# Scan layer: transposed input, ScalarE fills the bank of B, GpSimd keeps the states, a rewritten unit table

## The chip, the cores and the metric

The kernel runs on one core of one Trainium2 chip, and everything below is about that core. It has five engines that work side by side and wait for each other through semaphores: TensorE (PE; PEld is its weight load), VectorE (DVE), ScalarE (ACT), GpSimd (POOL) and SyncE (SP). In this kernel SP issues every DMA, so its queue is the order of all transfers. Matrix products are written to PSUM, which has 8 banks of 2 KB for each of 128 partitions; all else lives in SBUF and in device memory. The metric is the device time of one execution in microseconds (us).

## The reference

The input x has 8 sequences of 1024 rows of 256 numbers, all in float32. The computation, cut to what matters:

```
hs, res = split(x @ w_in.T)                      # 512 + 512 channels
u  = silu(causal_conv(hs, 4 taps))
dt, B, C = split(u @ w_xproj.T)                  # 64, 16, 16
delta = softplus(dt @ w_dt.T + b_dt)
z_t = exp(delta*A) * z_(t-1) + (delta*u) * B_t   # 512 channels x 16 states
y  = sum over states (z * C) + u*D
x1 = layernorm(x + (y * silu(res)) @ w_out.T)

q, k, v = x1 @ W_qkv + b_qkv                     # 16 heads of 16
attn = softmax(q k.T / 4) v
gate = softmax(x1 @ W_gate + b_gate); the two largest of 8 experts
moe  = sum over chosen experts of gate_e * (x1 @ W_e + b_e)
out  = layernorm(x1 + attn + moe)
```

## The kernel before

There are two parts, one after the other. `scan_moe_layer` computes everything but the attention and leaves `acc` (x1 plus experts), q and k (split in an upper half `hi` and a remainder `lo`) and v in device memory. `attention_layer` reads them. The change lies in the first part alone, and line numbers below are those of the kernel before.

**Steps, quads, slots.** The scan part works in 16 steps; a step is half a sequence, 512 rows. In a step there are 4 chunks of 128 channels and 16 states; with them 128 partitions hold 4 groups of 32 channels, and a *quad* is one of 16 combinations of a chunk and a state group g (in the order 0, 2, 1, 3). A quad has four scans of 128x512 (r = 0 to 3). One scan is one *slot*, so a step has 64 slots. Steps come in pairs: in the opening step the states start at zero, and the last column of each quad is kept in `state` (L649) for the closing step.

**What a quad does.** ScalarE makes the exponentials `da`, two slots ahead (L570, three PSUM buffers). `times_b` multiplies the 128x2048 input `ex` by the rows of B: for g below 2 on VectorE (L579), with B in a PSUM bank `pb`; for the others on GpSimd (L581), with B in the SBUF tile `bt`. VectorE scans (L630). GpSimd multiplies by the rows of C, `ct` (`times_c`, L586), in place, so the last column must have been copied before. TensorE sums the states two quads later (L596), and at the end of a chunk VectorE applies the gate (L603). `pb` is filled by TensorE (`copy_b`, L545): a 0/1 matrix `rp` picks rows of B out of `xd`. `pb` has one buffer, so the product waits for the multiply that reads it. `bt` and `ct` are filled by DMAs that repeat one row over 32 partitions, four for each tile (`load_bc`, L555); their buffers are single, so a load waits for the last reader of the step before.

**The table of units.** Everything else is cut into units, each a few products into one of three PSUM banks and a *read* some slots later (mostly two), which empties the bank. `SLOTS` (L46) says which unit starts at which of the 64 slots; the order of instructions on PE, ACT, DVE and POOL is exactly that of the program, while SP's is set by a scheduler. Units of the next step: `ph`, `pc`, `px`, `pd`, `pr` (projections, convolution, rows of B and C, delta, gate) and `pt`, which transposes the rows of x by TensorE and ScalarE (L188, L197) for `ph` and `pr`. Units of the step before: `po` (output projection and row norm; GpSimd's part L320 to L323), `yt` (transpose of x1), `pg` (gate logits), `q`, `v`, `gt` and `bi` (gate weights transposed, expert bias), and `e0` to `e15` (experts, two at a time, L487), whose read adds the product times the gate weight `gcb` on VectorE (L495). The gate's path is: VectorE takes `gmx` from `pg` and ScalarE copies it to `lg` (L414, L415), ScalarE's four exponentials `gex`, VectorE's comparisons `gp` (L422), GpSimd (L427, L428), VectorE's count `grk` (L431), and GpSimd's `gcb` (L436), nine slots after `pg`. For q and k, ScalarE writes `hi` (L363) and VectorE `lo` (L364) in the same read.

Of the kernel before, what the change touches and what calls it, by code (L numbers as in the profile page):

```python
# [16 lines left out]
P = 128  # L17
# [28 lines left out]
SLOTS = """  # L46
ph1 e12 ph2 e13 ph3 e14 e15 po0
po1 po2 po3 - - pc0 pc1 -
- - - yt0 yt1 pr0 pr1 pg
- q0 q1 v0 v1 pc2 pc3 q2  # L50
- px0 px1 q3 e0 pd0 pd1 gt
- e1 bi0 e2 bi1 pd2 pd3 e3
- e4 e5 e6 - pr2 pr3 e7
- e8 e9 pt0 pt1 e10 e11 ph0
""".split()
# [3 lines left out]
def scan_moe_layer(  # L59
    ctx, tc, ident, x, w_in, w_conv, w_x, w_dt, b_dt, a_log, d_skip, w_out, sel, rep,  # L60
    w_gate, b_gate, w_exp, b_exp, w_qkv, b_qk, acc, qk, v,
# [40 lines left out]

    def load_x(i, tag):

        b, s = steps[i]
        pool = p1 if tag == "xp" else p2
        t = work[i][tag] = pool.tile([P, TT, H], F32, tag=tag, name=f"{tag}_{b}_{s}")
        nc.sync.dma_start(t, x[b, s * LT : (s + 1) * LT, :].rearrange("(t p) h -> p t h", p=P))

    load_x(0, "xp")  # L110

    wi = wp.tile([P, HK, 2 * DIN], F32, name="wi")
    nc.sync.dma_start(wi, w_in.rearrange("(k p) d -> p k d", p=P))

# [3 lines left out]
    sl = wp.tile([P, ND], F32, name="sl")  # L118
    nc.sync.dma_start(sl, sel)

    wx = wp.tile([P, CH, R + 48], F32, name="wx")
# [14 lines left out]
    nc.sync.dma_start(wo, w_out.rearrange("(c p) h -> p c h", p=P))  # L136

    rp = wp.tile([R + NS, 2, P], F32, name="rp")
    nc.sync.dma_start(rp[R : R + NS].rearrange("n g p -> n (g p)"), rep)

# [21 lines left out]
    nc.gpsimd.memset(one, 1.0)  # L162

    be = rp[0:NE].rearrange("n g p -> n (g p)")
    nc.sync.dma_start(be, b_exp)
# [16 lines left out]
    def bank(name):  # L182
        return ps_m.tile([P, LT], F32, tag="mm", name=name)

    def transposed(name, xt, k):
        pt = bank(name)
        for t in range(TT):
            nc.tensor.transpose(pt[:, t * P : (t + 1) * P], xt[:, t, k * P : (k + 1) * P], ident)  # L188
        return pt

    def unit_pt(i, k):

        o = work[i]
        pt = transposed(f"pt_{i}_{k}", o["xp"], k)
        if k == 0:
            o["xT"] = p1.tile([P, HK, LT], F32, tag="xT", name=f"xT_{i}")
        yield 2, lambda: nc.scalar.copy(o["xT"][:, k, :], pt)  # L197

# [136 lines left out]
    def unit_yt(i, k):  # L335

        b, s = steps[i]
        o = work[i]
        pt = transposed(f"yt_{i}_{k}", o["xf"], k)
        if k == 0:  # L340
            o["yT"] = p1.tile([P, HK, LT], F32, tag="yT", name=f"yT_{i}")

        def read():
            nc.scalar.copy(o["yT"][:, k, :], pt)

        yield 2, read

    def unit_q(i, n):

        b, s = steps[i]  # L350
        o = work[i]
        c, a = divmod(n, 2)
        pq = bank(f"pq_{i}_{n}")
        for k in range(HK):
            nc.tensor.matmul(  # L355
                pq, wr[:, k, a * H + c * P : a * H + (c + 1) * P], o["yT"][:, k, :], start=(k == 0), stop=(k == HK - 1)
            )

        def read():
            hi = p4.tile([P, LT], F32R, tag="st", name=f"hi_{i}_{n}")  # L360
            lo = p4.tile([P, LT], F32R, tag="st", name=f"lo_{i}_{n}")
            bias = bqk[:, a, c : c + 1]
            nc.scalar.activation(hi, pq, AF.Identity, bias=bias)  # L363
            nc.vector.scalar_tensor_tensor(lo, pq, bias, hi.bitcast(F32), ALU.add, ALU.subtract)  # L364
            for j, t in ((0, hi), (1, lo)):
                nc.sync.dma_start(qk[b][c][a, :, j, s * LT : (s + 1) * LT], t.bitcast(F32))

        yield 2, read

    def unit_v(i, t2):  # L370
# [22 lines left out]
    def unit_pg(i, _):  # L393
# [18 lines left out]

        def logits():
            nc.scalar.copy(lg, pg)  # L414
            nc.vector.tensor_reduce(mx, pg, AX.X, ALU.max, negate=True)  # L415

# [86 lines left out]

    ahead = {"pt": unit_pt, "ph": unit_ph, "pc": unit_pc, "px": unit_px, "pd": unit_pd, "pr": unit_pr}
    behind = {
# [5 lines left out]
    def slot(t):  # L511
        i, j = divmod(t, len(SLOTS))
        if j == 8 and 0 < i + 2 < NSTEPS:
            load_x(i + 2, "xp")
        if j == 2 and 0 < i <= NSTEPS:
            load_x(i - 1, "xf")
        for read in due.pop(t, ()):
# [4 lines left out]
        if name in ahead:  # L522
            m = i + 2 if name in ("pt", "ph") and j >= 56 else i + 1
            if 0 <= m < NSTEPS:
                reads = ahead[name](m, n)
        elif name in behind:

            m = i - 2 if name == "e" and j < 16 else i - 1
            if 0 <= m < NSTEPS:
                reads = behind[name](m, n)  # L530
        for later, read in reads:
            due.setdefault(t + later, []).append(read)

    def place(k):
# [4 lines left out]
    def copy_b(k):  # L541

        i, c, g, o = place(k)
        pb = quads["b", k] = ps_b.tile([P, LT], F32, tag="pb", name=f"pb_{k}")
        nc.tensor.matmul(pb, rp[R : R + NS, g, :], o["xd"][R : R + NS, :], start=True, stop=True)  # L545

    def load_bc(i, g):

        o = work[i]
        for a, tag in ((0, "bt"), (1, "ct")):  # L550
            if a == 1 or g > 1:
                t = o[tag, g] = p1.tile([P, LT], F32, tag=f"{tag}{g}", name=f"{tag}_{i}_{g}")
                for m in range(NM):
                    row = o["bc"][a, 4 * m + g : 4 * m + g + 1]
                    nc.sync.dma_start(t[ND * m : ND * m + ND], row.to_broadcast([ND, LT]))  # L555

# [49 lines left out]
    with tc.manual_schedule(engines={eng.PE, eng.Activation, eng.DVE, eng.Pool}):  # L606
# [3 lines left out]
        for g in ORDER:  # L610
            load_bc(0, g)
        load_chunk(0, 1)
        load_experts(0)
        copy_b(0)
        times_b(0)
        copy_b(2)
        times_b(1)
        exp(0)
        exp(1)
        for k in range(K + 2):  # L620
            i, cj = divmod(k, QUADS)
            if cj > 12 and i + 1 < NSTEPS:
                load_bc(i + 1, ORDER[cj - 13])
            if cj == 0 and 0 < i < NSTEPS:
                load_bc(i, ORDER[3])
            for r in range(NR):
# [17 lines left out]
                if r == 3:  # L644
                    if k % 2 == 0 and k + 4 < K:
                        copy_b(k + 4)
                    if k < K:
                        if steps[i][1] + 1 < NSTEP:
                            nc.scalar.copy(state[:, c, g, :], quads[k][:, :, LT - 1])  # L649
                        times_c(k)  # L650
                slot(NR * k + r)
        for t in range(NR * (K + 2), len(SLOTS) * (NSTEPS + 1) + 18):
            slot(t)
# [255 lines left out]
def tile_kernel(  # L909
    ctx: ExitStack, tc, x, w_in, w_conv, w_x, w_dt, b_dt, a_log, d_skip, w_out, sel, rep,  # L910
    w_qkv, b_qk, b_v, w_gate, b_gate, w_exp, b_exp, out,
# [12 lines left out]
    scan_moe_layer(  # L924
        tc, ident, x, w_in, w_conv, w_x, w_dt, b_dt, a_log, d_skip, w_out, sel, rep,
        w_gate, b_gate, w_exp, b_exp, w_qkv, b_qk, acc, qk, v,
# [42 lines left out]
```

## Time and profile before

| | |
|---|---|
| median of 4 runs (lowest to highest) | 4028.35 us (4009.29 to 4036.53) |
| the profiled execution | 4021.62 us, its span 4019.6 us |
| scan part | the first scan starts at 77.5 us, the last ends at 2103.2 us |
| one step, opening / closing | 127.4 / 128.6 us in the middle of the part |
| attention part | from about 2188 us to the end |

The page's first rows give busy time, share of the span and instruction count of each engine:

```profile
PE 3656.7 (91%) x15168; PEld 1399.0 (35%) x15168; DVE 3219.1 (80%) x3590; ACT 2329.2 (58%) x3146; POOL 2062.7 (51%) x817
```

These shares mix the two parts. The change is to be judged by the rows of the scan part alone, which a table by window gives. In a row of waits, "A <- B: 62.6, 39, 2.6" says that A's engine sat idle 62.6 us in total, 39 times, at most 2.6 us, and that B ended the idle time. A timeline row has start, duration, engine, line and tiles, and in brackets the idle time before it.

### The profile page before, as it was taken

The page shows a single profiled execution, that of the slowest core. Times are in us where ns is not written, and L with a number is a line of the kernel's source. Part 1 is how long each engine was busy: PE and PEld are TensorE (multiplying, and loading weights), DVE is VectorE, ACT ScalarE, POOL GpSimd, SP SyncE. Part 2 cuts the span into 40 slices and gives each one's busy share as a digit, 9 for nine tenths or more (in the row PEclk, how much of TensorE's full clock was granted, in tenths as well). Part 3 has the DMA queues.
Part 4 walks back from the last instruction along what each step waited for, and adds up shares of the span by engine and source line. Part 5 has one row for each costly group of instructions (what it writes and reads, how often), then busy time and mean ns, then how long its engine had stood idle before and what let it go on. Part 6 is the DMA issues. An engine that isn't in the chain of part 4 may idle for free.

```text
span 4019.6 us, 45008 instructions
## 1 busy us (share of the span) xinstructions
PE 3656.7 (91%) x15168; PEld 1399.0 (35%) x15168; DVE 3219.1 (80%) x3590; ACT 2329.2 (58%) x3146; POOL 2062.7 (51%) x817
## 2 busy tenths in 40 slices
PE   5789898998989989898887899999999999999997
PEld 1133333333333333333334233333333333333332
DVE  2888998989989999899984577777777767777774
ACT  3656656655565556655540366666666656666665
POOL 2998999889998989889981000101101010101011
PEclk7689998999998999998987699999999989999999
DMA  8677776877677777777633322323323232323220
GB/s 209 145 185 191 179 190 173 198 188 188 173 182 195 184 192 173 197 189 173 170 82 118 99 75 85 90 94 89 99 80 111 74 102 79 106 85 94 89 77 27
DMA packets 288473, 545.51 MB, mean 136 GB/s; under 512 B 50459, under 2 KB 143795, under 8 KB 288243
## 3 DMA queue, kind: packets, MB, share of 16 engines
q1 hardware_dynamic: 288242, 542.63, 52.1%
q8 instruction: 121, 1.98, 0.2%
q14 instruction: 110, 0.89, 0.1%
HBM read 431.26 MB, written 110.15 MB: 135 GB/s over the span
## 4 chain that ended last, share of the span: by engine, by line
PE 47%; ACT 13%; DVE 13%; POOL 11%; DMA 7%; issue 6%; SPq 2%; ACTq 0%; POOLq 0%; DVEq 0%
PE av L819 13%; ACT es L802 11%; PE sc L800 11%; DVE dz L630 8%; POOL dz L586 8%; PE sm L775 7%; PE pe L487 3%; DMA ex<-dl 2%; PE y L596 2%; PE pq L355 2%; DVE dz L579 2%; DVE xf L495 2%; DMA hx<-hd 2%; POOL dz L581 1%; PE pr L202 1%
## 5 line engine op out<-in xcount | busy, mean ns | idle before, releaser
L779 DVE TENSOR_REDUCE mh<-sm 128x2 f32<-128x1024 f32 x1024 | 1250.0, 1223 | 395.5 <-PE sm L775 376.7
L802 ACT ACTIVATE es<-sc 128x1024 f32<-128x1024 f32 x1024 | 1047.2, 1024 | 660.0 <-PE sc L800 626.2
L586 POOL TENSOR_TENSOR dz<-dz,ct 128x2048 f32<-128x2048 f32 x256 | 1159.6, 4535 | 141.4 <-ACT state L649 78.2
L570 ACT ACTIVATE da<-ex,am 128x512 f32<-128x512 f32 x1024 | 698.0, 688 | 536.1 <-DVE dz L630 529.2
L844 POOL TENSOR_TENSOR acc<-acc,ot 128x256 f32<-128x256 f32 x64 | 46.7, 730 | 1464.4 <-DVE ot L840 1464.4
L800 PE MATMUL sc<-qst,kst 66*128 66x512 f32 x2048 | 763.2, 456 | 22.0 <-DMA qst<-mr 16.7
L630 DVE TENSOR_TENSOR_SCAN dz<-da,state,dz 128x512 f32<-128x512 f32 x512 | 630.5, 1267 | 11.6 <-ACT da L570 11.6
L630 DVE TENSOR_TENSOR_SCAN dz<-da,dz 128x512 f32<-128x512 f32 x512 | 599.1, 1207 | 17.7 <-ACT da L570 15.4
L581 POOL TENSOR_TENSOR dz<-ex,bt 128x2048 f32<-128x2048 f32 x128 | 580.2, 4533 | 36.6 <-DMA ct<-bc 32.5
L775 PE MATMUL sm<-kmx,qmx 64*128 64x512 f32 x2048 | 526.2, 511 | 54.3 <-DMA qst<-qk 10.7
L819 PE MATMUL av<-es,vaug 128*32 128x512 f32 x4096 | 559.2, 618 | 0.0
L487 PE MATMUL pe<-we,yT 128*128 128x512 f32 x1024 | 504.2, 628 | 37.1 <-ACT du L277 16.7
L800 PEld LDWEIGHTS sc<-qst,kst 66*128 66x128 f32 x2048 | 311.7, 191 | 587.6 <-DVE mh L779 299.7
L596 PE MATMUL y<-dz,sl 128*32 128x512 f32 x2048 | 311.9, 684 | 57.7 <-POOL dz L586 57.7
L775 PEld LDWEIGHTS sm<-kmx,qmx 64*128 64x128 f32 x2048 | 196.1, 188 | 457.2 <-ACT es L802 246.8
L579 DVE TENSOR_TENSOR dz<-ex,pb 128x2048 f32<-128x2048 f32 x128 | 289.8, 2264 | 67.9 <-DMA bt<-bc 63.5
L487 PEld LDWEIGHTS pe<-we,yT 128*128 128x128 f32 x1024 | 188.9, 196 | 324.3 <-issue 234.5
L495 DVE SCALAR_TENSOR_TENSOR xf<-pe,gcb,xf 128x256 f32<-128x256 f32 x512 | 243.4, 476 | 38.1 <-PE pe L487 29.0
L545 PE MATMUL pb<-xd,rp 16*128 16x512 f32 x256 | 161.6, 714 | 91.9 <-DVE dz L579 91.9
L202 PE MATMUL pr<-xT,wi 128*128 128x512 f32 x256 | 133.3, 668 | 2.2 <-ACT du L277 2.2
L355 PE MATMUL pq<-yT,wr 128*128 128x512 f32 x256 | 134.7, 664 | 0.0
L596 PEld LDWEIGHTS y<-dz,sl 128*32 128x32 f32 x2048 | 43.3, 114 | 251.0 <-issue 147.1
(106 smaller groups left out, 2751.7 us busy)
## 6 DMA issues: line engine op xcount, KB each, us to landing
ex<-dl SPq DMA_DIRECT2D x256, 512.0 KB
hx<-hd SPq DMA_DIRECT2D x256, 256.0 KB
we<-in_w_exp SPq DMA_DIRECT2D x130, 256.0 KB
dl<-du SPq DMA_DIRECT2D x64, 512.0 KB
qmx<-qk SPq DMA_DIRECT2D x128, 256.0 KB
kmx<-qk SPq DMA_DIRECT2D x256, 128.0 KB
qst<-qk SPq DMA_DIRECT2D x256, 128.0 KB
kst<-qk SPq DMA_DIRECT2D x512, 64.0 KB
```

The source lines that it names most:

```text
L487: nc.tensor.matmul(pe, o["yT"][:, k, t * P : (t + 1) * P], weights[e2][:, k].rearrange("p e f -> p (e f)"), start=(k == 0), stop=(k == HK ...
L570: nc.scalar.activation(da, o["ex", c][:, r, 0, :], AF.Exp, scale=am[:, c, g, r : r + 1])
L579: nc.vector.tensor_mul(t, o["ex", c][:, :, 1, :], quads.pop(("b", k)).unsqueeze(1).to_broadcast(full))
L581: nc.gpsimd.tensor_mul(t, o["ex", c][:, :, 1, :], o["bt", g].unsqueeze(1).to_broadcast(full))
L586: nc.gpsimd.tensor_mul(t, t, o["ct", g].unsqueeze(1).to_broadcast([P, NR, LT]))
L596: nc.tensor.matmul(y[ND * r : ND * r + ND, :], sl, t[:, r, :], start=False, stop=True, skip_group_check=True)
L630: nc.vector.tensor_tensor_scan(t[:, r, :], da, t[:, r, :], 0.0 if steps[i][1] == 0 else state[:, c, g, r : r + 1], ALU.mult, ALU.add,)
L775: nc.tensor.matmul(s[:, hh, :], qt_[rows, t * P : (t + 1) * P], kt_[rows, kh * QB : (kh + 1) * QB], start=True, stop=True,)
L779: nc.vector.tensor_reduce(mh[:, :, t, kh], s, AX.X, ALU.max)
L800: nc.tensor.matmul(s[:, cols], kt_[:, hh, kt * P : (kt + 1) * P], qt_[:, hh, cols], start=True, stop=True)
L802: nc.scalar.activation(e, s, AF.Exp, scale=HD**-0.5)
L819: nc.tensor.matmul(av[32 * j : 32 * j + 32, :], va[:, kt, VW * h : VW * h + 32], es[hh][:, q * QB : (q + 1) * QB], start=(kt == 0), stop=( ...
```

## The change

1. The host passes x a second time, transposed (`x_t`). `xT` is loaded by one DMA of 512 KB for each step, at slot 56 of the step before (`load_xt`); the units `pt`, their 8 transposes and 2 ScalarE copies, and the tile `xp` are gone. The load of `xf` (the residual rows) stays.
2. `copy_b` is a ScalarE copy of a tile `bt` into `pb`. So `bt` exists for all four g, `load_bc` is called for one tile at a time, and eight more row DMAs are issued in a step (`LOADS`: B's g 0 at quad 11, B's g 1 and C's g 0 at quad 13, and so on). The copy stands at odd quads, two slots ahead of its multiply, where TensorE's product stood six slots ahead. `rp` is gone.
3. The last states are copied by GpSimd (`tensor_copy`) just ahead of its own `times_c`.
4. In `unit_q`, `lo` and the two stores come one slot after `hi`; the tiles are taken when the unit starts. In `unit_pg`, `gmx` comes ahead of `lg`.
5. The table is rewritten: e0 starts at slot 31 instead of 36, e1 to e12 two to six slots later, e13, e14, e15 at slots 11, 15 and 17 instead of 3, 5 and 6; the units q and v are spread over slots 25 to 41; `gt`, `bi0`, `bi1` go from 39, 42, 44 to 42, 50, 52.
6. `w_in` is loaded in two halves at the start, and the loads before the first scan are reordered.

```
 SLOTS = """
-ph1 e12 ph2 e13 ph3 e14 e15 po0
-po1 po2 po3 - - pc0 pc1 -
-- - - yt0 yt1 pr0 pr1 pg
-- q0 q1 v0 v1 pc2 pc3 q2
-- px0 px1 q3 e0 pd0 pd1 gt
-- e1 bi0 e2 bi1 pd2 pd3 e3
-- e4 e5 e6 - pr2 pr3 e7
-- e8 e9 pt0 pt1 e10 e11 ph0
+ph1 e10 ph2 e11 ph3 e12 - po0
+po1 po2 po3 e13 - pc0 pc1 e14
+- e15 - yt0 yt1 pr0 pr1 pg
+- q0 v0 q1 - pc2 pc3 e0
+- px0 px1 v1 q2 pd0 pd1 -
+- q3 gt e1 - pd2 pd3 e2
+- e3 bi0 e4 bi1 pr2 pr3 e5
+- e6 e7 - e8 - e9 ph0
...
+    def load_xt(i):
+        b, s = steps[i]
+        t = work[i]["xT"] = p1.tile([P, HK, LT], F32, tag="xT", name=f"xT_{b}_{s}")
+        nc.sync.dma_start(t, x_t[b, :, s * LT : (s + 1) * LT].rearrange("(k p) t -> p k t", p=P))
...
-    def unit_pt(i, k):
-        o = work[i]
-        pt = transposed(f"pt_{i}_{k}", o["xp"], k)
-        if k == 0:
-            o["xT"] = p1.tile([P, HK, LT], F32, tag="xT", name=f"xT_{i}")
-        yield 2, lambda: nc.scalar.copy(o["xT"][:, k, :], pt)
...
         def read():
-            hi = p4.tile([P, LT], F32R, tag="st", name=f"hi_{i}_{n}")
-            lo = p4.tile([P, LT], F32R, tag="st", name=f"lo_{i}_{n}")
-            bias = bqk[:, a, c : c + 1]
             nc.scalar.activation(hi, pq, AF.Identity, bias=bias)
+
+        def rest():
             nc.vector.scalar_tensor_tensor(lo, pq, bias, hi.bitcast(F32), ALU.add, ALU.subtract)
...
         yield 2, read
+        yield 3, rest
...
         def logits():
+            nc.vector.tensor_reduce(mx, pg, AX.X, ALU.max, negate=True)
             nc.scalar.copy(lg, pg)
-            nc.vector.tensor_reduce(mx, pg, AX.X, ALU.max, negate=True)
...
-        if j == 8 and 0 < i + 2 < NSTEPS:
-            load_x(i + 2, "xp")
+        if j == 56 and 0 < i + 2 < NSTEPS:
+            load_xt(i + 2)
...
-            m = i - 2 if name == "e" and j < 16 else i - 1
+            m = i - 2 if name == "e" and j < 24 else i - 1
...
+    LOADS = ((11, 0, 0), (13, 0, 2), (13, 1, 0), (14, 0, 1), (14, 1, 1), (15, 1, 2))
...
-        nc.tensor.matmul(pb, rp[R : R + NS, g, :], o["xd"][R : R + NS, :], start=True, stop=True)
+        nc.scalar.copy(pb, o["bt", g])
...
-            if cj > 12 and i + 1 < NSTEPS:
-                load_bc(i + 1, ORDER[cj - 13])
+            if i + 1 < NSTEPS:
+                for at, a, j in LOADS:
+                    if cj == at:
+                        load_bc(i + 1, a, ORDER[j])
...
-                    if k % 2 == 0 and k + 4 < K:
-                        copy_b(k + 4)
+                    if k % 2 and k + 3 < K:
+                        copy_b(k + 3)
                     if k < K:
                         if steps[i][1] + 1 < NSTEP:
-                            nc.scalar.copy(state[:, c, g, :], quads[k][:, :, LT - 1])
+                            nc.gpsimd.tensor_copy(state[:, c, g, :], quads[k][:, :, LT - 1])
                         times_c(k)
```

## The prediction

> **What bounds the kernel now.** I read the page's busy shares first, then busy time by window, then groups by line, the totals of waits, and the timeline of three engines. A step is 64 slots, one per scan; slot numbers below are places in the table. Steps come in pairs (opening, closing half of a sequence); one pair from the middle, then the 10 us in the opening one in which TensorE was granted half its clock:
>
> ```profile
> 1084.30:1211.70 127.40, 115.66 (x414) 47.35 (x413) 115.24 (x133) 78.46 (x133) 115.67 (x38) 0.93 0.76 186
> 1211.70:1340.30 128.60, 117.37 (x420) 47.26 (x419) 118.93 (x133) 76.88 (x117) 118.02 (x38) 0.93 0.75 186
> ...
> 1121.00:1131.30 10.30, 8.86 (x22) 3.16 (x23) 9.06 (x9) 8.69 (x18) 10.30 (x4) 0.50 1.05 212
> ```
>
> The columns are stretch, length, then busy PE, PEld, DVE, ACT, POOL, granted clock, DMA share, GB/s. Three engines are busy 115 to 119 of 128 us: VectorE idles 12.2 and 9.7 us a step, GpSimd 11.7 and 10.6, TensorE 11.7 and 11.2. ScalarE idles 50. So no engine's work can be cut for its own worth; what counts is whose waits end last. Waits over 12.5 steps (360 to 1960 us):
>
> ```profile
> POOL dz L586 <- ACT state L649: 67.4, 26, 4.2
> DVE lo L364 <- ACT hi L363: 62.6, 39, 2.6
> PE pb L545 <- DVE dz L579: 61.3, 12, 5.5
> ...
> DVE gmx L415 <- ACT lg L414: 31.4, 13, 3.3
> ...
> DVE xf L495 <- PE pe L487: 12.3, 23, 0.7
> ...
> ACT hi L363 <- PE pq L355: 10.3, 6, 1.7
> ```
>
> ```profile
> 1120.95 1.98 PE L545 MATMUL pb<-xd,rp 16*128 16x512 f32 x2 [4.58 <-DVE dz L579]
> ```
>
> VectorE waits 5.0 us a step for `hi` and 2.5 for `lg`, and no row names GpSimd. Both waits stand in slots 25 to 33, and ScalarE is late there because TensorE is: it sat still 4.58 us at slot 18 (the line above: the product into `pb` waited for VectorE's multiply), dropped to half clock, and ran `pr`, `pg`, `pq` late. GpSimd's waits are for VectorE.
>
> What the new table will lean on is GpSimd's run from the end of the scan of slot 27 (1268.2) to the gate weights `gcb`, and VectorE's run to slot 33 beside it:
>
> ```profile
> 1268.22 4.53 POOL L586 TENSOR_TENSOR dz<-dz,ct 128x2048 f32<-128x2048 f32 x1 [0.19 <-DVE gsm L426]
> 1272.70 0.73 POOL L427 TENSOR_TENSOR gp<-gp,lower 128x256 f32<-128x256 f32 x1
> 1273.51 0.72 POOL L428 TENSOR_TENSOR gp<-gp 128x256 f32<-128x256 f32 x1
> 1274.19 4.55 POOL L581 TENSOR_TENSOR dz<-ex,bt 128x2048 f32<-128x2048 f32 x1
> 1278.69 4.56 POOL L586 TENSOR_TENSOR dz<-dz,ct 128x2048 f32<-128x2048 f32 x1
> ...
> 1283.80 0.25 POOL L436 TENSOR_TENSOR gcb<-grk,gex 128x32 f32<-128x32 f32 x1
> ```
>
> ```profile
> 1279.99 2.26 DVE L579 TENSOR_TENSOR dz<-ex,pb 128x2048 f32<-128x2048 f32 x1
> 1284.41 0.75 DVE L364 SCALAR_TENSOR_TENSOR lo<-pq,bqk,hi 128x512 fp32r<-128x512 f32 x1 [2.16 <-ACT hi L363]
> ```
>
> `gcb` is there 16.0 us after that scan. VectorE reaches the end of slot 33's multiply at 1282.25, 14.1 us after it, of which 3.1 us are waits (2.53 for `hi`, 0.43 for an exponential): 11.0 us of work.
>
> **The change, part by part, for one step.**
>
> *TensorE loses work.* Gone are 8 `pb` products (two passes each, 1.05 to 1.12 us together: 8.7) and 8 transposes of x (two units of four, 0.66 to 1.12 each: 1.8): 10.5 of 116.5 us. Experts e13 to e15 now lie at slots 11, 15 and 17, in the very hole in which TensorE stood still. So `pg` should end about when VectorE asks for it at slot 25, and the 2.4 us wait there goes. What is late next is ScalarE, for the comparison of slot 26. From the end of the scan of slot 23 it needs an exponential 0.75, table load 1.28, two Silus 1.2, table load and exponential 1.97, `lg` 0.2, exponential 0.7 and the gate's four 1.1: 7.2. VectorE needs two scans 2.4, the multiply 2.2, `gmx` 0.1 and a scan 1.2, and is there at 5.8: it waits 1.4 us, against 0.3 now (`lg` behind `gmx` costs nothing, ScalarE comes later anyway). Gain 1.3.
>
> *`lo` one slot later.* The three large `hi` waits (2.3 to 2.6) disappear as such, because a scan and ScalarE's queue lie between. `pq`'s bank is held a slot longer and q0, q1 stand two slots apart, so the ring of three banks still turns.
>
> *e0 moves from slot 36 to 31*, its VectorE read from 38 to 33. That read needs `gcb`, which GpSimd's queue gives 16.0 us after the scan of slot 27; VectorE's work up to there is 11.0. So VectorE waits 5.0 us at slot 33 (5.6 in opening steps, with two state copies in the run). Queued behind it are all scans, hence ScalarE's exponentials and TensorE's q2. This takes the place of what the `hi` waits gave: today slot 33's `lo` ends 17.1 us after the scan of slot 27, in the new order e0 may start after 16.0 to 16.6. GpSimd in turn stands still 3.3 us from `gcb` to the scan of slot 35 (e0 0.9, two scans 2.4), now as then (3.56).
>
> *State copies to GpSimd.* 16 in each opening step. ScalarE pays 0.193 for one; on GpSimd I bound it by its cheapest and dearest rows of 128x4: 0.20 (L322) and 1.04 (L321). It is a plain copy, nearest to L320's 0.23, plus 0.07 between dependent instructions: 0.30. From `gcb` to `gcb` there are 8 of them, 2.4 us. GpSimd's stretch becomes 3.3 + 116.8 + 1.3 (small gaps) + 2.4 = 123.8. It loses the wait for ScalarE (5.4 us a step), but that was mostly VectorE's lateness passed on.
>
> *`pb` by ScalarE.* 8 copies of 128x512, between 0.58 (L197) and 0.69 (L570, which writes the same kind of bank); 0.65. Less 2 copies of `xT` and in the mean 8 state copies (2.7): +2.5 of 78 us, hidden by 50 idle. The copy stands two slots (2.4 us of scans) before its multiply; without that cover VectorE would pay 8 x 0.65 = 5.2. Its rows `bt` 0 and 1 are asked for at slots 44 and 52, ten slots ahead.
>
> *SP.* 8 more row DMAs of 0.45 us, 3.6 us. `xT` is issued behind `ct`'s load, which waits for GpSimd's product of slot 55 (SP sits 5.3 us for that now, until 1205.7); it would land near 1211 to 1212, and ph0 is due at about 1210.6: 0 to 1.5 us of TensorE's slack.
>
> *The clock.* The 5 us wait at slot 33 empties TensorE around slots 35 to 39 (`q2` waits for e0's bank, `pd` for `xd`); I count `y` 1.1, `q2` 2.0 and `pd` 1.0 in 6.8 us there. At slot 43 of odd steps now, 5.0 busy of 6.8 were followed by 3.4 us at half clock; at slot 17, 2.0 to 4.5 by 10 to 13.7 us. So I expect the dip to move rather than go. A 3.4 us dip costs 1.7 us of product time and, with about 2 us slack a row, 1.0 us of VectorE's time (0 to 2.7).
>
> The Trainium skill, "TensorE: Matmul & The Clock Gate", Part 1, says that the array falls to half rate after an idle window of about 3.4 us. The trace shows its unit of 3.41 us, but a dip with 5.0 of 6.8 us busy, which the rule would not give. By the rule there is no gap that long left and the sum would be 15 us lower; I follow the rows.
>
> *Sum of a step.* VectorE's work 117.1 (unchanged), waits 5.3 + 1.4 + 1.0 (clock) + 1.0 (what stays of 3.0 us of small waits: `pe` 1.5, exponentials 1.0, `y` 0.4) = 125.8, against 128.0: 2.2 less, and 2.0 above GpSimd's 123.8. Fifteen steps: -33.
>
> *Start.* Step 0 is GpSimd's (102.4 of 109.2 busy): 16 x 0.30 = +4.8. Eight more row loads stand before the second chunk, 0 to +3.7; the transposes and the split `w_in` save about 1.5 before the first store. +4.5 (0 to 8.5). *End.* Two more expert units after the last scan, 3.8 us, fall into a 4.4 us hole (waiting for the normalized rows at 2123): 0. The attention part is untouched.
>
> -28.5 on the profiled execution's 4021.6 is 3993; that execution lies 6.7 below the median of the runs, so 4000.
>
> **Rivals.**
> 1. *GpSimd paces it, slower.* If a state copy costs 1.04 + 0.07, the stretch is 3.3 + 118.1 + 8.9 = 130.3: +2.3 x 15 + 17.8 at the start, about 4080. It decides from 0.82 us a copy. The 0.20 to 0.24 of other small rows speak against it.
> 2. *No change.* The wait for `gcb` comes with a long dip: e1 late by 2.7 us instead of 1.0, GpSimd half a microsecond late at slot 27. Then 128 a step, about 4030. For it: from slot 11 to 27 GpSimd needs six products at 4.51, the row norms 1.75 and gaps, 29.2, with four copies 30.4; VectorE needs 16 scans 18.5, two multiplies 4.4, three experts 2.7, two `po` 1.9, the gate's 1.4, and waits 1.4: 30.3. GpSimd has no room.
> 3. *More gain.* No dip, no small waits: GpSimd's floor 123.8, with copies at 0.2 123.0: -63 to -75 and the start, 3955 to 3970. Against it: two engines that close rarely mesh.
> 4. *The move does nothing*, since `hi` waits for `pq`: the `lo` waits stay. They would be covered by the `gcb` wait.
>
> **How the numbers follow.** My case (3975 to 4015) 0.42, rival 3 0.10, rival 2 with 4 0.27, rival 1 and other ways to lose 0.21. Within 0.5% (20 us) is about what a measurement of this kernel can tell from none. Part of my case lies within it: faster 0.47, same 0.29, slower 0.24. The range 3948 to 4070 leaves out the end of rival 3 and the dear end of rival 1; the likeliest case's own is 3975 to 4015.
>
> **What would show it.** `xf` of e0 waiting about 5 us for GpSimd once a step; no wait of `gmx`; `gp` waiting over 1 us for `gex`; `lo` without waits; state copies of 0.2 to 0.3 us on GpSimd; the half clock at slots 35 to 43 instead of 17 to 25; steps of 125 to 126. I am wrong if the copies are dear, if `xf` doesn't wait at slot 33, or if TensorE's half clock stays at slot 17.

## The result and the profile after

The changed kernel takes 4046.8 us (median of 40 runs, 4012.8 to 4078.0), the kernel before 4025.0 in the runs beside it (66 runs, 4001.3 to 4087.7). The ratio is 1.0053, with a 95% interval from 1.0039 to 1.0066: half a percent slower, where 4000 was forecast. Runs more than 1.5% above the fastest of their kernel count in medians and ranges, but not in ratios.

The profiled execution spans 4033.9 us. Its first scan starts at 83.9 us (77.5 before) and its last scan ends at 2135.6 (2103.2 before). Of these 32.4 us, 6.4 come before the first scan, 4.4 in step 0, and 22.3 in steps 2 to 15 (step 1 gave 0.6 back). Behind the scan this execution then took 18 us less than the one before (1898 against 1916). This part varies by tens of microseconds from execution to execution (see the last section), so experiments are compared here by the last scan's end as well as by the time.

The windows of an opening and a closing step of the changed kernel (stretch, length, busy time of PE, PEld, DVE, ACT, POOL, granted clock, DMA share, GB/s; a step of the kernel before took 127.4 and 128.6 us at this place):

```profile
1106.00:1233.30 127.30, 107.78 (x391) 43.48 (x389) 115.06 (x133) 79.72 (x123) 118.03 (x53) 0.95 0.77 190
1233.30:1364.90 131.60, 113.29 (x394) 45.62 (x395) 118.53 (x132) 80.67 (x123) 118.15 (x39) 0.90 0.76 185
```

TensorE lost work (111.6 us busy a step, 116.2 before; means of steps 2 to 14), VectorE's is unchanged (116.6, 116.9), GpSimd's grew a little (118.2, 116.7). VectorE's idle time grew from 10.8 to 12.9 us a step (mean of steps 2 to 14), GpSimd's from 11.0 to 11.4. The totals of waits from 360 to 1960 us of the changed kernel (waiting instruction, what it waited for: us in all, times, longest):

```profile
DVE xf L488 <- POOL gcb L429: 61.5, 13, 5.2
PE pc L225 <- DMA hx<-hd: 53.7, 14, 7.8
...
DVE xf L488 <- PE pe L480: 39.0, 35, 3.7
POOL dz L576 <- DMA bt<-bc: 29.1, 8, 4.5
...
DVE xf L302 <- DMA xf<-in_x: 20.4, 10, 3.6
...
POOL dz L576 <- DMA ct<-bc: 17.1, 4, 4.9
...
DVE gp L415 <- ACT gex L412: 14.1, 13, 1.2
```

The first and the last line are the two waits that the prediction had put there; the waits of `lo` for `hi` fell from 62.6 to 6.2 us. The four lines that name `hx`, `xf`, `bt` and `ct` are loads, which the prediction had not priced (`hs`, the read of `ph`, is stored to device memory, and `hx` is loaded from there for the convolution `pc`): `pc` waited 5.7 us for `hx` before, GpSimd 11.2 for rows, and VectorE never for `xf`.

### The profile page after: what moved, and what is told of

It reads as the page before. It is cut to its first block, busy times and chain, and to the rows that moved or that the text cites. A ratio compares the mean times of both kernels' runs of the same rounds, so it can differ in the third digit from the quotient of the medians.

```text
span 4033.9 us, 44586 instructions
## 1 busy us (share of the span) xinstructions
PE 3543.7 (88%) x14784; PEld 1356.9 (34%) x14784; DVE 3215.3 (80%) x3590; ACT 2367.2 (59%) x3114; POOL 2084.2 (52%) x945
## 4 chain that ended last, share of the span: by engine, by line
PE 37%; POOL 22%; ACT 13%; DMA 11%; DVE 8%; issue 6%; SPq 3%; ACTq 0%; POOLq 0%; DVEq 0%
POOL dz L581 13%; PE av L819 13%; ACT es L802 11%; PE sc L800 10%; PE sm L775 7%; POOL dz L576 6%; DVE dz L630 6%; DMA ex<-dl 4%; DMA hd<-hs 3%; DMA hx<-hd 2%; PE pe L480 2%; POOL du L266 1%; DVE xf L488 1%; PE pr L190 1%; SPq L550 1%
## 5 line engine op out<-in xcount | busy, mean ns | idle before, releaser
L630 DVE TENSOR_TENSOR_SCAN dz<-da,dz 128x512 f32<-128x512 f32 x512 | 596.9, 1206 | 13.7 <-ACT da L565 11.3
L480 PE MATMUL pe<-we,yT 128*128 128x512 f32 x1024 | 520.4, 640 | 9.0 <-issue 2.5
L225 PE MATMUL pc<-hx,cw 128*32 128x512 f32 x512 | 82.7, 744 | 99.3 <-DMA hx<-hd 83.0
L348 PE MATMUL pq<-yT,wr 128*128 128x512 f32 x256 | 141.8, 681 | 22.7 <-ACT du L265 12.3
L190 PE MATMUL ph<-xT,wi 128*128 128x512 f32 x256 | 130.8, 639 | 34.2 <-DMA xT<-in_x_t 18.3
```

What stands on the lines that cost most here:

```text
L480: nc.tensor.matmul(pe, o["yT"][:, k, t * P : (t + 1) * P], weights[e2][:, k].rearrange("p e f -> p (e f)"), start=(k == 0), stop=(k == HK ...
L630: nc.vector.tensor_tensor_scan(t[:, r, :], da, t[:, r, :], 0.0 if steps[i][1] == 0 else state[:, c, g, r : r + 1], ALU.mult, ALU.add,)
```

## The predicted chain at slot 33

VectorE's and GpSimd's timelines of the changed kernel around slot 33 of a closing step (start, length, instruction, idle time before it and its releaser):

```profile
1302.92 2.26 DVE L574 TENSOR_TENSOR dz<-ex,pb 128x2048 f32<-128x2048 f32 x1
1309.99 1.00 DVE L488 SCALAR_TENSOR_TENSOR xf<-pe,gcb,xf 128x256 f32<-128x256 f32 x2 [4.81 <-POOL gcb L429]
```

```profile
1294.12 4.57 POOL L581 TENSOR_TENSOR dz<-dz,ct 128x2048 f32<-128x2048 f32 x1 [1.52 <-DVE gsm L419]
...
1309.70 0.25 POOL L429 TENSOR_TENSOR gcb<-grk,gex 128x32 f32<-128x32 f32 x1
1313.43 4.51 POOL L581 TENSOR_TENSOR dz<-dz,ct 128x2048 f32<-128x2048 f32 x1 [3.48 <-DVE dz L630]
```

The scan of slot 27 ends at 1294.05. `gcb` is there 15.9 us later (16.0 forecast), VectorE's work up to slot 33 ends 11.1 us later (11.0 forecast), and GpSimd then stands still 3.48 us (3.3 forecast). The state copies are cheap; the group of the changed kernel (nanoseconds: least, median, most):

```profile
L649 POOL COPY state<-dz x128: 177/187/217, 90.7 to 2016.3; 128x4 f32<-128x4 f32 x128
```

The product into `pb` is gone from TensorE, and its wait of 4.58 us at slot 18 with it. What TensorE stands for at about the same place now, in the changed kernel's timeline:

```profile
1270.05 1.94 PE L225 MATMUL pc<-hx,cw 128*32 128x512 f32 x8 [7.03 <-DMA hx<-hd]
```

So the parts of the forecast that came out of compute rows hold here to 0.2 us. The miss is elsewhere.

## Experiments

Starts and ends (us) are from one profiled execution of each kernel; times and ratios are from its runs, against the kernel before run beside it (medians of 4025 to 4029). Set against the kernel before, the ratio turned into microseconds and the last scan's end agree to 15 us in every row (changed kernel 21 and 32), so a few microseconds between single ends decide nothing.

| kernel | first scan | last scan's end | time, median | ratio, 95% interval |
|---|---|---|---|---|
| before | 77.5 | 2103.2 | 4025.0 | 1 |
| changed | 83.9 | 2135.6 | 4046.8 | 1.0053 (1.0039 to 1.0066) |
| x1: xf early | 83.4 | 2113.2 | 4037.3 | 1.0030 (1.0005 to 1.0056) |
| x2: xf and xT early | 81.7 | 2111.5 | 4036.7 | 1.0018 (0.9994 to 1.0042) |
| x3: e0 later | 83.0 | 2089.0 | 4004.8 | 0.9940 (0.9921 to 0.9960) |
| x4: state copies on ScalarE | 83.0 | 2115.5 | 4038.6 | 1.0027 (1.0003 to 1.0051) |
| x5: x2 and rows apart | 84.9 | 2091.5 | 3998.0 | 0.9937 (0.9909 to 0.9965) |
| x6: x5 and e0 later | 83.6 | 2057.4 | 3972.5 | 0.9851 (0.9814 to 0.9889) |
| x7: before, lo later | 78.4 | 2115.4 | 4031.1 | 1.0015 (0.9986 to 1.0045) |
| x8: changed, old table | 82.8 | 2130.4 | 4051.6 | 1.0065 (1.0041 to 1.0089) |
| x9: x6, state copies on ScalarE | 84.6 | 2051.6 | 3973.5 | 0.9860 (0.9819 to 0.9901) |
| x10: changed, pb by TensorE | 79.7 | 2129.4 | 4043.2 | 1.0057 (1.0036 to 1.0077) |
| x11: before, rows apart | 76.7 | 2095.3 | 4020.8 | 0.9987 (0.9966 to 1.0008) |
| x12: before, xT alone | 81.2 | 2099.4 | 4020.8 | 0.9984 (0.9955 to 1.0012) |
| x13: changed, rows apart | 82.3 | 2096.4 | 4023.1 | 0.9986 (0.9953 to 1.0018) |
| x14: x6, other start | 83.1 | 2047.6 | 3966.8 | 0.9868 (0.9833 to 0.9903) |

Two theories stood first. G: the 4.7 us wait at slot 33 sets the step. L: late loads do.

**x1, `xf` asked for early**

```
-        if j == 2 and 0 < i <= NSTEPS:
-            load_x(i - 1)
+        if j == 36 and 0 <= i < NSTEPS:
+            load_x(i)
```

> The changed kernel, with the load of x for the residual rows (xf, 512 KB) asked for at slot 36 of the cycle before, ahead of the stores of B and C, as SyncE issued it in the kernel before; in the changed kernel it is issued at slot 0 to 9 of its own cycle, between the stores hs and the loads hx. Theory L (late loads): the 22 us that steps 2 to 15 lost come from this queue. VectorE's wait of its po read for xf (1.57 us a step) goes, hx lands earlier, PE pc's wait for hx (53.7 us in 360 to 1960) falls under 25, the wait of the expert read at slot 17 (1.28) falls under 0.6; steps 1.5 to 3 us shorter, last scan's end 2135.6 minus 22 to 45, the time 4046.8 minus 20 to 45, that is 4002 to 4027. Theory G (the wait of 4.7 us for the gate weights at slot 33 sets the step, other waits lie inside GpSimd's pace): the po wait goes, the wait at slot 33 grows by as much, the last scan's end stays within 8 us of 2135.6.

The scan ended 22.4 us earlier, at the near edge of what theory L said (22 to 45); the time, 4037.3, missed its 4002 to 4027. The `po` read no longer waits. But `pc` still waits 36.1 us for `hx` (under 25 was expected), the expert read at slot 17 still 1.5 us, and GpSimd 48.3 us for rows. The load `xf` is one part of it only.

**x2, `xT` early too**

```
-        if j == 56 and 0 < i + 2 < NSTEPS:
+        if j == 54 and 0 < i + 2 < NSTEPS:
             load_xt(i + 2)
```

> As the run before (xf asked for at slot 36), and the transposed x (xT, 512 KB) asked for at slot 54 instead of 56, ahead of the rows bt and ct of the second and third groups instead of behind ct's. Theory L: xT lands 3 to 4 us earlier, PE ph's wait for xT (18.3 us on the page) goes, hs is stored 1 to 2 us earlier; the rows behind it land later by what 512 KB take, so the gain over the run before is small: last scan's end 0 to 10 us earlier than there. Theory G: no change from the run before.

1.7 us earlier than x1; `ph` no longer waits for `xT` in the window, and that gains next to nothing: `pc`'s wait for `hx` is back at 46.5 us, and GpSimd's for rows is 50.6. Both theories allowed so small a gain.

**x3, the first expert unit at slot 39**

```
-- q0 v0 q1 - pc2 pc3 e0
-- px0 px1 v1 q2 pd0 pd1 -
+- q0 v0 q1 - pc2 pc3 -
+- px0 px1 v1 q2 pd0 pd1 e0
```

> The changed kernel with the first expert unit at slot 39 (a blank) instead of 31, so that VectorE asks for the gate weights at slot 41, after GpSimd has them; slot 31 is left blank. Theory G: the wait at slot 33 (4.7 us a step) goes and nothing of its size takes its place; steps 2 to 4 us shorter, last scan's end 2135.6 minus 30 to 60, the time 3990 to 4017. Theory L or a pace set by GpSimd: the 4.7 us go to other waits (gate's later waits, po's read for xf, pe at slots 17 and 57); the last scan's end moves by less than 10 us. Slot 31 blank leaves TensorE idle 1.3 us longer there; a dip of the clock at slots 31 to 38 would show it.

The scan ended 46.6 us earlier and the kernel is faster than both. The wait for `gcb` is gone, and with it GpSimd's stand of 3.4 us at slot 36, which is caused by it: GpSimd waits there for scans that are queued behind the waiting expert read. Of the 4.7 us, 1.8 come back: `pe` at slot 41 is new (1.6), `lo` waits 2.1 at slots 39 and 44 against 0.3 at slot 28, and `pe` at slots 57 and 59 loses its 1.6. Theory G holds for this part of the time; it does not tell why the forecast, which had the wait in it, was too low.

**x4, the state copies back on ScalarE**

```
-                            nc.gpsimd.tensor_copy(state[:, c, g, :], quads[k][:, :, LT - 1])
+                            nc.scalar.copy(state[:, c, g, :], quads[k][:, :, LT - 1])
```

> The changed kernel with the copies of the last states back on ScalarE (0.193 us each there in the profile before; 0.189 on GpSimd in the profile after, 16 in each opening step, with their gaps about 0.26). If these copies are what GpSimd pays for: step 0 shorter by 16 x 0.26 = 4.2 us, and opening steps by up to 4.2, seven of them: last scan's end 2135.6 minus 4 to 33. If the step is set elsewhere: step 0 alone gets its 4.2 back, and GpSimd's product waits for ScalarE again (67 us in 360 to 1960 before, 26 times): the end within 8 us of 2135.6.

20.1 us earlier, 3.4 of it in step 0 and 14.7 in steps 2 to 15, although GpSimd again waits for ScalarE (43.5 us). So in the changed kernel GpSimd's time counts; by the ratios the gain is about 10 us, with intervals that overlap.

**Where GpSimd loses it.** GpSimd's product of a step's fourth group, the first that needs `bt` 3, can start 12.5 us after the step's first scan (x11 and x13, without a wait). In steps 3 to 13 it started 13.9 us after it in the kernel before (mean of eleven) and 16.9 in the changed one: 3.0 us a step. SyncE's queue shows why. The queue of the kernel before, around the start of step 7 at 955.7:

```profile
949.75 1.69 SPq L555 DMA_DIRECT2D ct<-bc  x4
951.54 0.90 SPq L473 DMA_DIRECT2D we<-in_w_exp  x2
954.25 1.72 SPq L555 DMA_DIRECT2D ct<-bc  x4
956.07 1.80 SPq L561 DMA_DIRECT2D ex<-dl  x4
957.91 1.99 SPq L555 DMA_DIRECT2D bt<-bc  x4
963.24 6.78 SPq L555 DMA_DIRECT2D ct<-bc  x4
970.12 0.37 SPq L225 DMA_DIRECT2D hd<-hs  x1
```

The queue of the changed kernel, around the start of step 7 at 973.9:

```profile
970.55 0.39 SPq L113 DMA_DIRECT2D xT<-in_x_t  x1
973.50 1.70 SPq L550 DMA_DIRECT2D ct<-bc  x4
975.30 0.90 SPq L466 DMA_DIRECT2D we<-in_w_exp  x2
976.30 1.84 SPq L556 DMA_DIRECT2D ex<-dl  x4
978.19 2.91 SPq L550 DMA_DIRECT2D bt<-bc  x4
983.80 7.13 SPq L550 DMA_DIRECT2D ct<-bc  x4
...
991.49 0.38 SPq L213 DMA_DIRECT2D hd<-hs  x1
991.91 0.43 SPq L107 DMA_DIRECT2D xf<-in_x  x1
```

The load `bt` in these lines is the fourth group's. It is issued 2.2 us after the step's start before and 4.3 after the change. What pushed it: `ct` 1 ahead of it waits for a GpSimd product and came 1.1 us later; the expert weights `we`, which the new table asks for at slot 60 instead of 57, now lie between. Behind it stands `ct` 3, which waits until GpSimd has finished with its buffer (a product that ends at 982.7) and whose issue then takes 7.13 us for what took 1.70 two loads earlier; `hs`, ready 2.4 to 2.9 us into the step, is stored only behind it, at 15 to 18 us (12 to 14 before), and `xf` behind that. The GpSimd products in question, before and after:

```profile
970.70 4.53 POOL L581 TENSOR_TENSOR dz<-ex,bt 128x2048 f32<-128x2048 f32 x1 [2.43 <-DMA ct<-bc]
```

```profile
991.70 4.54 POOL L576 TENSOR_TENSOR dz<-ex,bt 128x2048 f32<-128x2048 f32 x1 [4.47 <-DMA bt<-bc]
```

The late product is not the whole loss. In x1 it starts as late, 17.0 us into the step in the mean; its line in step 7, which starts there at 967.4:

```profile
984.58 4.55 POOL L576 TENSOR_TENSOR dz<-ex,bt 128x2048 f32<-128x2048 f32 x1 [3.91 <-DMA ct<-bc]
```

And yet x1's scan ended 22.4 us earlier, with VectorE's wait for `xf` gone (1.6 us a step in the changed kernel). The same queue makes two engines late: GpSimd by `bt` 3, VectorE by `xf`.

**x5, the fourth group's rows apart, on top of x2.** `bt` 3 is asked for ahead of `ct` 1, and `ct` 3, which is used at slot 15, at slot 4.

```
-    LOADS = ((11, 0, 0), (13, 0, 2), (13, 1, 0), (14, 0, 1), (14, 1, 1), (15, 1, 2))
+    LOADS = ((11, 0, 0), (13, 0, 2), (13, 1, 0), (14, 0, 1), (14, 1, 1), (15, 0, 3), (15, 1, 2))
...
-            if cj == 0 and 0 < i < NSTEPS:
-                for a in range(2):
-                    load_bc(i, a, ORDER[3])
+            if cj == 1 and 0 < i < NSTEPS:
+                load_bc(i, 1, ORDER[3])
```

> As x2_x_early (xf and xT asked for early), and the fourth group's rows apart: the load of bt 3 asked for at slot 60 of the cycle before, ahead of ct 1, instead of at slot 0; the load of ct 3, which is used at slot 15, at slot 4 instead of 0, behind the first stores hs. In x2's profile SyncE's queue stood behind that ct load (it waits for GpSimd's product of slot 63), so hs was stored at slot 9 and hx loaded 20 to 25 us after the step's start, against 17 to 23 in the kernel before; GpSimd waited 4.2 us a step at slots 7 to 9 for rows. Theory P (GpSimd's loop sets the step, and late rows are what lengthened it): its row waits fall under 1.5 us a step, PE pc's wait for hx (46.5 us in 360 to 1960) under 15, the expert read at slot 17 waits under 0.7 us (1.97); steps of 123.5 to 125.5, last scan's end 2060 to 2087 (2111.5 in x2), the time 3985 to 4012. Theory G (the 5 us wait at slot 33 sets the step by itself): row waits go, but steps stay at 127 to 128.5 and the end at 2103 to 2115.

The end is 44.1 us before the changed kernel's (20.0 before x2's) and the time 3998.0, faster than before, with the wait at slot 33 still there. GpSimd waits for no row in the window. Steps are 125.2 and 127.4 us by turns, 126.3 in the mean (123.5 to 125.5 was expected; the end missed by 4.5 us what was expected of it). `pc` still waits 24.4 us for `hx`. VectorE's waits of x5:

```profile
DVE xf L488 <- POOL gcb L429: 56.8, 13, 5.2
DVE xf L488 <- PE pe L480: 17.4, 12, 2.8
DVE gp L415 <- ACT gex L412: 13.1, 13, 1.2
DVE lo L356 <- ACT hi L353: 11.6, 23, 1.2
```

**x6, both mended:** x5 with the table of x3.

> As x5_x_rows, with the first expert unit at slot 39 as in x3_e0_later (which ended its last scan at 2089.0). If loads and the wait at slot 33 cost separately: GpSimd stands still neither for rows nor at slot 36 (3.45 us), steps of 120.5 to 123.5, last scan's end 2025 to 2060, the time 3950 to 3985. If one hides the other: as the better of x3 and x5, within 8 us. If TensorE's clock takes over: pe waits at slots 17, 41 and 57 of over 4 us a step together, steps near 124 to 126.

78.2 us earlier than the changed kernel, most of the sum of x3 and x5 (46.6 and 44.1), though steps of 122.9 to 125.8 stay above what was hoped. 1.5% faster than the kernel before. Its pair from the middle:

```profile
1070.20:1193.10 122.90, 109.12 (x383) 45.11 (x382) 114.86 (x133) 79.75 (x123) 117.30 (x53) 0.92 0.78 195
1193.10:1318.70 125.60, 114.31 (x405) 46.05 (x404) 118.51 (x132) 79.97 (x123) 118.90 (x39) 0.92 0.80 195
```

**x7, the kernel before with `lo` an entry later and `gmx` first**

```
         def read():
             nc.scalar.activation(hi, pq, AF.Identity, bias=bias)
+        def rest():
             nc.vector.scalar_tensor_tensor(lo, pq, bias, hi.bitcast(F32), ALU.add, ALU.subtract)
...
         yield 2, read
+        yield 3, rest
...
```

> The kernel before with two parts of the change alone: lo an entry later, the maximum ahead of the copy of the logits. VectorE waited 5.0 us a step for hi and 2.5 for lg. If VectorE's waits set the step of the kernel before: lo's waits of over 2 us fall to 0.6 or less and steps become 2 to 4 us shorter, last scan's end 2103.2 minus 30 to 60, the time 4027 minus 30 to 60. If GpSimd's loop sets it: the waits go from lo to other places (GpSimd's stand of 3.6 us at slots 11 and 36 stays), the end within 12 us of 2103.2.

No gain: the end 12.2 us later, the time the same. The wait only moved. VectorE's waits of x7:

```profile
DVE lo L366 <- ACT hi L363: 54.6, 19, 4.5
DVE gmx L417 <- PE pg L405: 33.0, 13, 3.0
```

`lo` now waits up to 4.5 us at slot 34, and ScalarE's `hi` waits 34.5 us in all (never before) for the store of an earlier `hi`. The reading is that the ring of four staging buffers is held longer while the old table asks for `q` units too closely; that was not tried by itself. `gmx` waits as long for `pg` as it did for `lg`, so there it was `pg` that came late, as the prediction reckoned.

**x8, the changed kernel with the old table**, its slots for the transposes blank.

```
+ph1 e12 ph2 e13 ph3 e14 e15 po0
+po1 po2 po3 - - pc0 pc1 -
+- - - yt0 yt1 pr0 pr1 pg
+- q0 q1 v0 v1 pc2 pc3 q2
+- px0 px1 q3 e0 pd0 pd1 gt
+- e1 bi0 e2 bi1 pd2 pd3 e3
+- e4 e5 e6 - pr2 pr3 e7
+- e8 e9 - - e10 e11 ph0
...
```

> The changed kernel with the table of units of the kernel before, its two transpose slots left blank, so that all parts of the change but the table are in: the first expert unit at slot 36, e12 to e15 at slots 1 to 6. No wait for the gate weights. If the table is what lost: last scan's end under 2095 and the time under 4015. If the loads are (rows ahead of hs, xT behind ct): the end stays at 2100 to 2130, with GpSimd's waits for rows of 3 us or more a step; the store of acc at slot 8 instead of 19 lets xf be loaded earlier.

No wait for `gcb`, yet as slow as the changed kernel: `lo` waits 71.0 us for `hi`, up to 5.4, as in x7. So neither expectation was right in its reason. Whether the new table is better as a whole can't be judged by this run, only that `lo` later goes badly with the old one's `q` units. But of the loads it decides something. GpSimd's product on `bt` 3 starts 14.3 us into the step in the mean (13.9 in the kernel before, 16.9 in the changed one), GpSimd waits 17.3 us for rows instead of 46.2, and VectorE never for `xf`. Its line in step 7, which starts at 972.0:

```profile
987.05 4.53 POOL L576 TENSOR_TENSOR dz<-ex,bt 128x2048 f32<-128x2048 f32 x1 [2.13 <-DMA ct<-bc]
```

All other parts of the change are in, the eight row loads and `xT` too. So it is the new table that makes the queue late.

**x9, the state copies on ScalarE in x6** (the edit of x4).

> As x6_x_rows_e0 (loads early, rows apart, first expert unit at slot 39), with the state copies on ScalarE. In x4 the same step took 20 us off the changed kernel's last scan. If GpSimd's work still sets the step (it is busy 117 to 118 of 123 to 126 us in x6): 16 x 0.26 = 4.2 us less in each opening step, last scan's end 2057.4 minus 10 to 30, the time 3972 minus 5 to 30. If VectorE's chain sets it (busy 115 to 119, waits 8 to 10): within 8 us of 2057.4; GpSimd's products wait for ScalarE's copies instead (43.5 us in 360 to 1960 in x4).

5.8 us earlier, the time the same within its interval. Where neither rows nor `gcb` stop GpSimd, the copies' place matters little.

**x10, the rows of B by TensorE's product in the changed kernel**

```
-        nc.scalar.copy(pb, o["bt", g])
+        nc.tensor.matmul(pb, rp[R : R + NS, g, :], o["xd"][R : R + NS, :], start=True, stop=True)
...
+        if a == 0 and g < 2:
+            return
```

> The changed kernel with the rows of B in the bank by TensorE's product again, as in the kernel before: no rows bt 0 and 1 are loaded (8 DMAs a step fewer), no copies on ScalarE. Theory D (the 8 more row loads make the queue late): hx lands earlier, PE pc's wait for hx (53.7 us in 360 to 1960) falls under 25, GpSimd's waits for rows (46.2 us) under 20, last scan's end 2135.6 minus 15 to 35. Theory X (the place of the loads xf and xT in the queue does it, x1_xf_early took 22 us off): little changes there, the end within 10 us of 2135.6; and the product waits again for VectorE's multiply (61 us in 360 to 1960 before), which adds 0 to 15.

The first scan starts 4.2 us earlier, and steps 2 to 15 gain 1.0 us in all. Kernels whose start is that of the changed one begin between 81.7 and 84.9, so 2 to 5 us of the start go to the row loads and the copies behind them. `pc`'s wait for `hx` stays at 51.4, GpSimd's for rows falls from 46.2 to 31.5 and VectorE's for `xf` from 20.4 to 6.2; but `lo` waits 18.7 instead of 6.2 and `pe` 46.8 instead of 39.0, and the step stays as long. The eight row loads have a part in the lateness, but taking them out does not shorten the steps.

**x11, the kernel before with the fourth group's rows apart** (the edit of x5 in its own loops).

> The kernel before with the fourth group's rows apart, as in x5: bt 3 at slot 60 ahead of ct 1, ct 3 at slot 4. In the kernel before GpSimd waits 0.8 us a step for rows and hx is loaded 17 to 23 us after the step's start. If the queue costs the kernel before nothing: last scan's end within 8 us of 2103.2 and the time within 12 of 4027. If it costs there too what it costs in the changed kernel (20 us between x2 and x5): 2080 to 2090, and the time 4005 to 4015; then x5's gain over the kernel before is not the change's own.

7.9 us earlier, the time the same. GpSimd's product on `bt` 3 starts 12.5 us into every step, and what it waited for rows it then waits at slot 11 for VectorE and ScalarE (3.6 us before, 4.5 to 5.8 in x11). So what the rows give in the changed kernel is not there to be had in the kernel before.

**x12, the kernel before with the transposed load alone**

```
-        if j == 8 and 0 < i + 2 < NSTEPS:
-            load_x(i + 2, "xp")
+        if j == 56 and 0 < i + 2 < NSTEPS:
+            load_xt(i + 2)
...
```

> The kernel before with the transposed load alone: xT loaded at slot 56 in place of the load xp at slot 8 and the eight transposes with their two copies; the table's two slots blank. If the place of xT behind ct 2's load makes ph late: PE ph waits for xT, hs is stored later, hx later; last scan's end 2103.2 plus 5 to 20. If it only takes TensorE's 1.8 us away and frees SyncE at slot 10: the end within 8 us of 2103.2, less about 1.5 us at the start.

3.8 us earlier at the end, although the first scan came 3.7 later. In the kernel before, the transposed load does no harm.

**x13, the rows apart alone in the changed kernel** (the edit of x5, without x2's).

> The changed kernel with the fourth group's rows apart (bt 3 at slot 60 ahead of ct 1, ct 3 at slot 4), and the loads xf and xT left where the change has them. In x5, with xf and xT early as well, the last scan ended 44.1 us before the changed kernel's 2135.6; xf and xT alone (x2) gave 24.1, so the rows gave 20.0 behind them. If the two act apart: 2135.6 minus 15 to 25. If the rows are late only because SyncE's queue is jammed by xf: less than 8 us off. If GpSimd's wait for rows is the larger loss in any order: minus 30 to 45, and xf's load then costs nothing.

39.2 us earlier with two loads moved (27 by the ratios, 1.0053 to 0.9986); `xf` and `xT` add 4.9 behind that. SyncE's queue of x13 around the start of step 7 at 957.5, and its GpSimd product:

```profile
953.35 1.86 SPq L550 DMA_DIRECT2D bt<-bc  x4
955.85 1.69 SPq L550 DMA_DIRECT2D ct<-bc  x4
957.64 0.91 SPq L466 DMA_DIRECT2D we<-in_w_exp  x2
958.65 1.83 SPq L556 DMA_DIRECT2D ex<-dl  x4
...
961.66 1.24 SPq L213 DMA_DIRECT2D hd<-hs  x1
962.94 0.61 SPq L107 DMA_DIRECT2D xf<-in_x  x1
```

```profile
969.99 4.54 POOL L576 TENSOR_TENSOR dz<-ex,bt 128x2048 f32<-128x2048 f32 x1
```

The product starts 12.5 us into the step without waiting. `xf` is still issued after the step's start, but no longer behind `ct` 3, and VectorE does not wait for it. So x13 ends both waits, and its 39.2 us hold both effects: `xf` and `xT` asked for early gain 24.1 by themselves (x2), the two row loads 20.0 more (x5). Which of the two, `bt` 3 or `ct` 3, does how much was not tried.

**x14, another order of the first loads in x6**

```
+        load_bc(0, 0, ORDER[0])
         load_chunk(0, 0)
...
+        exp(0)
         copy_b(0)
```

> x6_x_rows_e0 with another order at the start: the rows bt of the first group ahead of the first chunk ex, the second chunk ahead of the last rows of C, the first exponential ahead of the copies pb. In x6 the first scan starts at 83.6 (77.5 in the kernel before): ScalarE's first copy pb waited 15.1 us for bt until 78.0, and the first exponential came behind the second pb copy, which waited 2.35 us for VectorE's multiply. If this order is what the start costs: first scan 3 to 8 us earlier and step 0 0 to 5 us shorter, last scan's end 2057.4 minus 3 to 13, the time 3972 minus 3 to 13. If the rows land late for the DMA engines' load: first scan within 2 us of 83.6.

The first scan starts at 83.1, 0.5 us earlier, within the spread of equal starts: the order is not what the start costs. The end is 9.8 us earlier by steps 2 to 15, which the start does not explain; the time's interval overlaps x6's. What the start costs beyond the row loads and the state copies stays open.

## Why the prediction was wrong

- **The failed step** is the paragraph on SP. It priced the queue's change as 3.6 us of issue time and as `xT` landing 0 to 1.5 us into TensorE's slack, and gave the sum nothing for it. It looked at the loads that the diff adds and not at those that stand behind them. `bt` 3 came 2 us later into its step, the GpSimd product on it 3.0 us later, and this is a product on the engine of which the prediction itself says that it has no room. `xf`, a load that the diff leaves alone, came so late that VectorE waited 1.6 us a step for it. x13 moves two loads, ends both and takes 39.2 us off.
- **The sum of GpSimd's stretch**, 123.8, had 1.3 us for all small gaps. Waits for rows alone are 3.75 us a step after the change. GpSimd could not keep the 2.0 us margin under VectorE's 125.8.
- **VectorE's small waits** were put at 1.0, with 1.0 more for the clock. They are 7.1: of 12.9 us idle in a step 4.7 are `gcb` and 1.1 `gp`. Of the 7.1, 0.9 are gaps too short to be listed as waits, as much as in the kernel before. (The `pe` of 1.5 in the prediction's small waits is 1.0 by its own row, 12.3 us in 12.5 steps.) The largest are the read of `xf` at slot 9 (1.6), which x13 and x5 remove, and of `pe` at slots 17, 57 and 59 (2.9).
- **The account.** For steps 1 to 15 the prediction had 1916.5 - 33 = 1883.5 us; the changed kernel took 1938.2, x5 1894.8. So 43.4 of the 54.7 us missed are the loads, as far as x5's edits take them out. The remaining 11.3, 0.75 a step, are small waits in x5: `pe` 1.4, `lo` 0.9, `gmx` and `bi` 0.5 each, against 2.0 in the sum for small waits and the clock. That x5's time, 3998.0, meets the forecast of 4000 is in part luck: its scan ends at 2091.5, where the forecast's sum gives 2103.2 - 28.5 = 2074.7, and in x5's profile the part behind the scan took 1888 us against 1916 in the kernel before.
- **Right in place and size:** the wait for `gcb` (4.7 us; 5.3 forecast), `gp` for `gex` (1.1; 1.4), the end of the `lo` waits, the copies' price (0.19 us; 0.30 taken) and that rival 1 would not happen. That the `gcb` wait would take the place of the `hi` waits without loss is not shown: x3 gains 46.6 us when it goes.
- **The start** was put at 4.5 us with 8.5 as its bound; it is 10.8 (6.4 to the first scan, 4.4 in step 0). x10 gives 2 to 5 of it to the row loads and their copies; x4, whose step 0 takes 110.2 us against 111.7 to 113.6 in kernels with the copies on GpSimd, gives 1.5 to 3.4 to the state copies.
- **The clock** did move, but to many places: dips begin for the most part at slots 9, 13 to 16, 25, 38, 49 and 53 (17, 25, 43 and 60 before). The one at slot 38 was forecast; that half the clock still stands at slots 15 to 17 was a sign of being wrong by the prediction's own list. From 360 us to the scan's end TensorE stood at half clock 270 us before, 328 after, 297 in x5 and 283 in x6. x6 is 1.5% faster than the kernel before with more of it, so it did not decide.
- **Rival 2** had the right size (128 us a step; 129.0 measured in steps 2 to 15), but it was argued by a long dip of the clock and half a microsecond of GpSimd, not by the queue.

What stays open: x8 shows that the table makes the loads late, but which of its moves does so was not tried one by one. Read from the queue, they are `we` at slot 60, which now lies ahead of `bt` 3, and the last experts, with which the store of `acc` goes out 47 to 51 us into the step instead of 24 to 26.

## What to carry to other kernels

A queue that issues in order is a resource like an engine: when a table moves, list for each load what stands ahead of it in the queue and what that waits for, above all the loads of a single buffer that an engine at its limit reads. A load whose buffer comes free late and whose data is used late belongs behind those that are needed at once. And an engine's wait for a result of another one is not free because an equal wait went: it also stops what is queued behind it, which here was the other engine's next input.

## What the runs showed of the hardware

- Four row loads of 64 KB each are issued in 1.7 us as a rule, but in 7.1 us where they follow the 512 KB of `we`, the 2 MB of `ex` and another row load; in the kernel before 6.8.
- After the scan, at the opening of the attention part, TensorE is granted half its clock in one stretch of 58 to 157 us, by kernel and execution (102 before, 65 in the changed kernel's profile, 157 in x13). From the scan's end to the end of the execution 1888 to 1935 us pass; less half of that and of the later stretches at half clock it is the same to 14 us in all sixteen profiles. By an estimate from these lengths, half of 157 less 58, up to 50 us of the spread between runs (65 us for the changed kernel) can come from there. Where the half clock lay in runs without a profile was not seen, but their mean granted clock falls as the time grows: 0.932 in the changed kernel's fastest run (4012.8), 0.913 in its slowest (4078.0). And the stretch does not end when TensorE is busy again; windows of x13:

```profile
2200.00:2240.00 40.00, 22.53 (x64) 7.75 (x62) 16.23 (x15) 8.18 (x8) 4.77 (x7) 0.50 0.52 151
2240.00:2280.00 40.00, 40.00 (x121) 12.50 (x113) 17.63 (x16) 15.11 (x16) 0.00 (x0) 0.50 0.14 43
2280.00:2320.00 40.00, 40.00 (x121) 13.38 (x117) 17.87 (x19) 15.12 (x16) 0.73 (x1) 0.50 0.17 53
2320.00:2360.00 40.00, 39.34 (x185) 14.35 (x177) 27.27 (x31) 22.21 (x23) 4.13 (x6) 0.90 0.25 72
```

For 80 us TensorE's matmuls fill the window at a granted clock of 0.50, 121 of them in 40 us against 185 in the next 40 at 0.90. The Trainium skill, "TensorE: Matmul & The Clock Gate", Part 1, has the full rate come back after one busy window of about 3.4 us; this stretch contradicts it, and the measurement decides.
